# The sort's hits of rank and slot: a PSUM tile and three products in place of an SBUF tile and one

## The chip, the cores and the metric

One Trainium2 chip, one core of it. The metric is the device time of one execution in microseconds; the number given is the median of three runs. One further execution was taken by the hardware profiler, and all durations of single instructions below are from that one.

## What is computed

A graph network of two layers over 12,500 nodes with 128 features and 200,000 edges of 8 relations, then a layer norm. The edges are sorted by their destination. Each layer is

```
W = einsum('rb,bio->rio', comp, basis)
xw = einsum('ni,rio->nro', x, W)
msgs = xw[src, et]
seg = dst * N_REL + et
summed = segment_sum(msgs, seg);  cnt = segment_sum(1, seg)
mean = summed / maximum(cnt, 1)
h_new = relu(mean.reshape(N_NODES, N_REL, HIDDEN).sum(axis=1) + x @ root + bias)
h = h_new + h
```

and the output is `_layernorm(x + h)`. All values are float32.

## The kernel before

The edges are cut into 1,563 tiles of 128, and eight tiles make a quad (196 quads). **Layer 0** (the loop `for o in range(NG - 3)`) works on a quad per iteration. GpSimd issues one indirect DMA for each tile (`gather`, L806), which fetches the 128 rows of `x` that the edges of this tile name; a few tiles (`SINGLES`) are fetched row by row from the SyncE queue instead. The ring of row tiles holds seven quads, and gathers are issued five quads ahead of the iteration that uses them. TensorE multiplies the rows with one-hot matrices of destination and weight (`means`, L1364), ScalarE copies the sums out, TensorE multiplies with the relations' weights (`product`, L1396) and places the rows in blocks of 128 nodes (`place`, L1427). **Layer 1** gathers rows of a table `y_d` that layer 0 has written.

In layer 1, 62 of the 196 quads (`ROUTED`, NR = 62) are not fetched by eight gathers but picked out of SBUF by one-hot matmuls, and only edges that find no room there are fetched by one gather for the quad. The lists for that are made in layer 0 by a counting sort, **the sort** of this text: 62 steps, one in each iteration from 96 on. The profile has them between 975 and 1601 us. A step handles 8 tiles of 128 edges. Every edge belongs to one of 32 groups, and each group has 32 slots (CAP). In an iteration the step's parts stand in this order on VectorE, behind the one-hot matrices of the quad (L1270, L1278):

- `ranks_of(x)`, L1666 to L1674: TensorE has left in the PSUM tile `ct`, 256 columns of it, how many earlier edges each group had (`earlier_of`, L1643 to L1645). L1666 and L1667 take from this the rank of each edge in its group, L1668 to L1670 mark those with no room, L1671 writes the **hits**, a one where slot number equals rank (8 tiles by 32 slots), and L1674 multiplies the hits with three values of the edge (8 by 3 by 32) into `v`.
- `lefts_of(x - 1)`, L1683 to L1686: the edges with no room, for the step before. It reads eight columns of `ct` behind the counts.
- `groups_of(x + 1)`, L1626 to L1630: the one-hot groups of the next step.

TensorE's part of the iteration ends with `earlier_of`, which writes `ct` anew, and `slots_of` (L1700, L1706), which multiplies the groups with `v` and the left-overs with their values into the PSUM tile `y`. VectorE's L1666 of the next iteration is queued behind all that VectorE has before it and needs the new `ct`.

The order on every engine is the order in which the code calls these functions. A planner (`Plan.add`) puts waits on semaphores in between, from the cells that each instruction reads and writes; a read of a PSUM tile counts as a write of it there. An instruction of VectorE waits for an earlier one of VectorE only where one of its cells asks for it. Nearly all small SBUF tiles of the sort lie in one large tensor, so the profile calls them all `arena`; `cols`, the column numbers that the comparisons use, lies in PSUM.

The lines that matter for the prediction are those of `ranks_of`.

Of the kernel before, what the change touches and what calls it, by code (L numbers as in the profile page):

```python
# [9 lines left out]
F16 = mybir.dt.float16  # L10
# [4 lines left out]
ALU = mybir.AluOpType  # L15
# [415 lines left out]
def ordered_path(  # L431
# [25 lines left out]
    nc = tc.nc  # L457
    P = 128
# [11 lines left out]
    Q = 8  # L470
# [23 lines left out]
    CAP = 32  # L494
# [101 lines left out]
    def part_of(n, *cell):  # L596
        nonlocal free_at
        free_at += n
        assert free_at <= at
        sort_c.append(cell)  # L600
        return arena[:, free_at - n:free_at], cell
# [3 lines left out]
    val_b = part_of(NV * 3, "val")  # L605
# [5 lines left out]
    v_b = [part_of(Q * 3 * CAP // 2, "v", i) for i in range(2)]  # L611
    h_at = free_at
    left_hot_b = [part_of(Q * P // 2, "left_hot", i) for i in range(2)]
    j_b = part_of(Q * CAP // 2, "j")
    count_b = part_of(Q * NGR, "count")
    rank_b, lv_b, top_b = part_of(Q, "rank"), part_of(Q, "lv"), part_of(Q, "top")
    lo_b = [part_of(CAP // 2, "lo", i) for i in range(2)]
# [37 lines left out]
    cols = bank[:, :P].bitcast(F16)  # L655
# [31 lines left out]
    def vec(emit, reads=(), writes=()):  # L687
        plan.add("DVE", emit, reads, writes)
# [20 lines left out]
    def in_turn(emits):  # L709
        def emit():  # L710
            for e in emits:
                last = e()
            return last

        return emit
# [812 lines left out]
    val = val_b[0].bitcast(F16).rearrange("p (n k v) -> p n k v", k=Q, v=6)  # L1528
# [77 lines left out]
    def hots_of(x):  # L1606
        o, oc = oh_b[x % 3]
        return o.bitcast(F16).rearrange("p (t g) -> p t g", g=NGR), oc
# [8 lines left out]
    def flags(x):  # L1617
        f, c = fl_b[x % 2]
        f = f.bitcast(F16)
        return f[:, 1:Q + 1], f[:, 11:11 + Q + 2], f[:, 22:22 + Q], f, c  # L1620
# [11 lines left out]
    def counts_in(b):  # L1632
        return b.rearrange("p t d -> p (t d)")[:, :Q * NGR].rearrange("p (t g) -> p t g", g=NGR)

    def before_in(b):
        return b.rearrange("p t d -> p (t d)")[:, Q * NGR:Q * NGR + Q]

    def earlier_of(x):
        b, bc = ct_b
        reads, emits = [tri_b[1], one_b[1]], []  # L1640

        def sums(at_b, one, two):
            nc.tensor.matmul(at_b, tri, one, start=True, stop=False)  # L1643
            nc.tensor.matmul(at_b[:, 1:], every, two[:, :Q - 1], start=False, stop=False)
            return nc.tensor.matmul(at_b[:, 5:], every, two[:, :Q - 5], start=False, stop=True)  # L1645

        if x < NR:
            (o3, oc), (r2, rc) = hots_of(x), run2(x)
            reads += [oc, rc]
            emits.append(lambda: sums(counts_in(b), o3[:, 1:], r2))  # L1650
        if x > 0:
            f0, _, f2, _, fc = flags(x - 1)
            reads.append(fc)
            emits.append(lambda: sums(before_in(b), f0, f2))
        pe(in_turn(emits), reads, [bc])

    def ranks_of(x):
        (o3, oc), (vv, vc), (jt, jc), (ct, cc) = hots_of(x), v_b[x % 2], j_b, count_b
        f0, f1, f2, fw, fc = flags(x)
        b, bc = ct_b  # L1660
        c3 = ct.rearrange("p (t g) -> p t g", g=NGR)
        b3 = counts_in(b)
        j3 = jt.bitcast(F16).rearrange("p (t c) -> p t c", t=Q)
        v4 = vv.bitcast(F16).rearrange("p (t v c) -> p t v c", t=Q, v=3)
        rk, rc = rank_b
        vec(lambda: nc.vector.tensor_tensor(c3, b3, o3[:, 1:], op=ALU.mult), [bc, oc], [cc])  # L1666
        vec(lambda: nc.vector.tensor_reduce(rk, c3, axis=AX.X, op=ALU.add), [cc], [rc])  # L1667
        vec(lambda: nc.vector.tensor_scalar(f0, rk, float(CAP), None, op0=ALU.is_ge), [rc], [fc])  # L1668
        vec(lambda: nc.vector.tensor_tensor(f1[:, 2:], f0, fw[:, :Q], op=ALU.add), [], [fc])
        vec(lambda: nc.vector.tensor_tensor(f2, f1[:, 2:], f1[:, :Q], op=ALU.add), [], [fc])  # L1670
        vec(lambda: nc.vector.tensor_tensor(  # L1671
            j3, cols[:, None, :CAP].to_broadcast([P, Q, CAP]), rk.unsqueeze(2).to_broadcast([P, Q, CAP]),
            op=ALU.is_equal), ["cols", rc], [jc])
        vec(lambda: nc.vector.tensor_tensor(  # L1674
            v4, j3[:, :, None, :].to_broadcast([P, Q, 3, CAP]),
            val[:, x, :, :3].unsqueeze(3).to_broadcast([P, Q, 3, CAP]), op=ALU.mult), [jc, val_b[1]], [vc])

    def lefts_of(x):
        f0, _, _, _, fc = flags(x)
        b, bc = ct_b  # L1680
        (lv, lc), (h, hc), (top, tc_) = lv_b, left_hot_b[x % 2], top_b
        h3 = h.bitcast(F16).rearrange("p (t c) -> p t c", t=Q)
        vec(lambda: nc.vector.scalar_tensor_tensor(lv, before_in(b), 1.0, f0, op0=ALU.add, op1=ALU.mult),  # L1683
            [bc, fc], [lc])
        vec(lambda: nc.vector.tensor_tensor(top, top, lv, op=ALU.max), [lc], [tc_])
        vec(lambda: nc.vector.tensor_tensor(  # L1686
            h3, cols[:, None, 1:P + 1].to_broadcast([P, Q, P]), lv.unsqueeze(2).to_broadcast([P, Q, P]),
            op=ALU.is_equal), ["cols", lc], [hc])
# [520 lines left out]
    def sup(q):  # L2209
        return (q * Q + G) // (2 * G) - 1  # L2210
# [104 lines left out]
    for o in range(NG - 3):  # L2315
# [17 lines left out]
        if 0 <= at_x - 1 < NR:  # L2333
            ranks_of(at_x - 1)
# [22 lines left out]
        if len(tables) > 4 and (TABLE <= o < SORT - 2 or o >= SORT + NR + 4):  # L2357
            a, b = tables.pop(0)(pt_b)
# [11 lines left out]
        for i in range(2):  # L2370
            if turned_to:
                here = pt_b
                a, b = turned_to.pop(0)
            elif tables and o >= TABLE and (i == 0 or len(tables) > 6 or o > NG - 16):
# [3 lines left out]
                a, b = tables.pop(0)(here)  # L2378
# [88 lines left out]
    for q in range(NQ):  # L2467
# [48 lines left out]
        for i in range(2):  # L2516
# [14 lines left out]
            elif i == 0:  # L2531
                for j in [late] * (0 <= late < FULL) + [q] * (q >= FULL):
                    if opened_by(j)[1]:
                        a, b = finish(1, sup(j))
# [11 lines left out]
def kernel(  # L2546
# [18 lines left out]
    flag = ctx.enter_context(tc.tile_pool(name="flag", bufs=1))  # L2565
    bad = flag.tile([1, 1], I32, name="bad")
    plan = ordered_path(tc, bad, x, src, dst, et, basis, comp, root, bias, out)
    every = [mybir.EngineType.PE, mybir.EngineType.Activation, mybir.EngineType.DVE, mybir.EngineType.Pool,
             mybir.EngineType.SP]
# [36 lines left out]
```

## Time and profile before

| | |
|---|---|
| runs, median of 3 | 3381.97 us (3380.82 to 3383.55) |
| profiled execution: its own time | 3385.05 us |
| profiled execution: span, first to last instruction | 3383.1 us |
| granted TensorE clock, mean of the span | 0.911 |
| layer 0's gathers: first start, last end | 4.58 us, 1950.34 us |
| the sort: first L1674, last L1674 | 977.3 us, 1592.5 us |

The profiled execution took 3.08 us more than the median of the runs, and 1.95 us more than its own span. Times in rows are microseconds from the start of the span, and durations are microseconds unless ns is said. A row of a group of instructions gives line, engine, operation, what it writes and reads with the shapes (partitions x elements, type), the count, then the busy time and the mean duration of one in ns, then the idle time of the engine ahead of them and what ended it. A row of the timeline gives start, duration, engine, line, operation and operands, and in brackets the idle time ahead of it.

### The profile page before, as it was taken

The numbers are of one execution on the slowest core, as the hardware profiler recorded it, in microseconds if no ns is written. First come the engines' busy times: TensorE is split into PE (matmuls) and PEld (weight loads), VectorE is DVE, ScalarE is ACT, GpSimd is POOL, SyncE is SP. The second block draws the span as 40 slices with busy tenths as digits, with TensorE's granted clock in tenths as the row PEclk, the third lists the DMA queues.
The fourth block names the chain that finished last, engine by engine and source line by source line (L and its number), as shares of the span: only waits on it lengthen the run. The fifth ranks groups of instructions, "written<-read, shape, count | busy, mean of one in ns | idle before, by whom it ended". The sixth has DMA issues, their size and how long they took to land.

```text
span 3383.1 us, 73915 instructions
## 1 busy us (share of the span) xinstructions
PE 2766.1 (82%) x27537; PEld 2228.2 (66%) x27537; DVE 2270.8 (67%) x6302; ACT 644.9 (19%) x1627; POOL 2547.9 (75%) x2677
## 2 busy tenths in 40 slices
PE   6777667877667777777776739999999999999995
PEld 4565565656566666766565627777777777777774
DVE  6665454463367888888333238888888888888884
ACT  1211112222122222222222211111111111111110
POOL 7777777777777777777777777777777777777775
PEclk8999879888888888888988879999999999999997
DMA  4242223443322232222333232233223322333222
GB/s 138 56 59 64 57 77 113 132 130 95 89 82 81 75 89 76 82 77 82 115 105 89 88 101 73 72 84 85 78 78 84 84 78 78 84 85 82 78 78 61
DMA packets 171649, 289.03 MB, mean 85 GB/s; under 512 B 66163, under 2 KB 102813, under 8 KB 171285
## 3 DMA queue, kind: packets, MB, share of 16 engines
q0 software_dynamic: 85408, 175.09, 20.3%
q1 hardware_dynamic: 47146, 50.19, 5.0%
q10 hardware_dynamic: 38731, 58.99, 4.9%
q8 instruction: 218, 3.57, 0.5%
q14 instruction: 146, 1.20, 0.1%
HBM read 218.35 MB, written 65.70 MB: 84 GB/s over the span
## 4 chain that ended last, share of the span: by engine, by line
PE 43%; POOL 40%; issue 13%; DVE 2%; DMA 2%; ACT 1%; POOLq 0%; ACTq 0%; SPq 0%; DVEq 0%
POOL rows L806 40%; PE pt L1918 11%; PE y L1938 9%; PE po L1938 7%; PE po L1958 3%; PE s L2059 3%; PE ct L2026 2%; PE s L1364 2%; PE y L1396 1%; DMA rows<-in_x_dram,idx 1%; PE s L2061 1%; DVE dm L1270 1%; PE s L2063 1%; DVE arena L999 1%; PE pt L1495 0%
## 5 line engine op out<-in xcount | busy, mean ns | idle before, releaser
L806 POOL DMA_INDIRECT rows<-in_x_dram,idx x1539 | 1476.8, 960 | 471.3 <-issue 463.5
L806 POOL DMA_INDIRECT rows<-y_d,idy x1067 | 1010.4, 947 | 325.1 <-issue 316.6
L1364 PE MATMUL s<-dm,rows 128*128 128x128 f32 x3078 | 531.6, 344 | 379.6 <-DMA rows<-in_x_dram,idx 351.8
L1364 PEld LDWEIGHTS s<-dm,rows 128*128 128x128 f32 x3078 | 495.2, 252 | 441.1 <-issue 228.1
L1270 DVE TENSOR_SCALAR dm<-cols,kr,w 128x128 f32<-128x128 f16 x1563 | 525.1, 400 | 194.7 <-PE pt L1495 54.8
L1396 PE MATMUL y<-w_sb,sT 128*128 128x128 f32 x3136 | 438.6, 299 | 46.4 <-ACT sT L704 46.4
L1396 PEld LDWEIGHTS y<-w_sb,sT 128*128 128x128 f32 x3136 | 424.6, 217 | 56.4 <-ACT sT L704 55.2
L1918 PE MATMUL pt<-arena,dm 128*32 128x128 f32 x12152 | 391.3, 275 | 2.8 <-DVE dm L1868 2.1
L704 ACT ACTIVATE sT<-s 128x512 f32<-128x512 f32 x391 | 212.3, 594 | 824.8 <-PE s L1364 824.8
L1918 PEld LDWEIGHTS pt<-arena,dm 128*32 128x32 f32 x12152 | 324.6, 110 | 55.2 <-issue 43.0
L1938 PE MATMUL y<-arena,dm 128*128 128x304 f32 x620 | 229.6, 452 | 35.1 <-DVE arena L1885 35.1
L1229 DVE TENSOR_SCALAR sT<-cols,kr,w 128x32 f32<-128x32 f16 x1040 | 238.1, 300 | 7.4 <-PE s L2063 7.3
L1868 DVE TENSOR_TENSOR dm<-arena,cols 128x768 f32<-128x768 f16 x248 | 231.3, 933 | 4.1 <-DMA dm<-sc_d 3.7
L1448 DVE TENSOR_TENSOR po<-po,carry 128x128 f32<-128x128 f32 x98 | 28.8, 294 | 296.9 <-PE pt L1495 104.2
L1938 PE MATMUL po<-arena,dm 128*128 128x304 f32 x620 | 210.3, 421 | 0.0
L704 ACT ACTIVATE dm<-pt 128x256 f32<-128x256 f32 x248 | 95.4, 385 | 578.2 <-PE pt L1918 533.6
L1495 PE MATMUL pt<-w_sb,arena 128*128 128x512 f32 (+1 forms) x326 | 174.5, 618 | 26.3 <-ACT y_row L704 14.9
L704 ACT ACTIVATE y_row<-pt 128x512 f32<-128x512 f32 x165 | 98.5, 597 | 417.8 <-PE pt L1495 153.3
L1938 PEld LDWEIGHTS y<-arena,dm 128*128 128x128 f32 x620 | 102.9, 189 | 88.4 <-DVE arena L1885 35.3
L1885 DVE TENSOR_SCALAR arena<-cols,comp_sb 128x608 f32<-128x608 f16 x155 | 134.9, 902 | 36.1 <-DMA arena<-y_d,arena 36.0
L1938 PEld LDWEIGHTS po<-arena,dm 128*128 128x128 f32 x620 | 118.4, 191 | 41.3 <-issue 0.7
L1885 DVE TENSOR_SCALAR arena<-cols,sel 128x608 f32<-128x608 f16 x155 | 134.8, 902 | 0.0
(327 smaller groups left out, 3583.5 us busy)
## 6 DMA issues: line engine op xcount, KB each, us to landing
hw_SP<-in_x_dram SPq DMA_DIRECT2D x3072, 0.5 KB
y_d<-y_row ACTq DMA_DIRECT2D x96, 512.0 KB
rows<-in_x_dram,idx POOLq DMA_INDIRECT x1539
rows<-y_d,idy POOLq DMA_INDIRECT x1067
arena<-lo_d SPq DMA_DIRECT2D x62, 256.0 KB
x_g<-in_x_dram SPq DMA_DIRECT2D x24, 512.0 KB
h_d<-arena ACTq DMA_DIRECT2D x96, 64.0 KB
out_dram<-x_g SPq DMA_DIRECT2D x12, 512.0 KB
```

Of the source, the lines that this page charges most:

```text
L704: act(lambda: nc.scalar.activation(out_t, in_t, AF.Copy), reads, writes)
L806: ins.append(nc.gpsimd.indirect_dma_start(out=t[:, i - q * Q, :], out_offset=None, in_=table_t, in_offset=bass.IndirectOffsetOnAxis(ap=ids ...
L1229: vec(in_turn([lambda i=i: nc.vector.tensor_scalar(t[:, i, :], cols[:, :2 * K], kr[:, i0 + i:i0 + i + 1], w[:, i0 + i:i0 + i + 1], op0=ALU ...
L1270: emits.append(lambda i=i: nc.vector.tensor_scalar(t[:, i - q * Q, :wide], cols[:, :wide], ids[:, i:i + 1], w[:, i:i + 1], op0=ALU.is_equa ...
L1364: last = nc.tensor.matmul(s_b[i // 4][0][:, i % 4, :], t[:, i, :] if one is None else one[0], d[:, i, :], start=True, stop=True)
L1396: last = nc.tensor.matmul(y[:m], t[:, r, :nt, :].rearrange("p t k -> p (t k)"), w_sb[:, 0, r, :], start=(r == 0), stop=(r == R - 1))
L1495: pe(lambda: nc.tensor.matmul(hb[:n].rearrange("p r d -> p (r d)"), hT[:, j * P:j * P + n], w_sb[:, 1, k * H:(k + 1) * H, :].rearrange("p ...
L1868: emits = [lambda: nc.vector.tensor_tensor(o[:, :3 * n].rearrange("p (j c) -> p j c", j=3), bits[:, None, u * n:(u + 1) * n].to_broadcast( ...
L1885: vec(lambda v=v, o=o: nc.vector.tensor_scalar(o, segs_p, sg[:, v:v + 1], sg[:, NTL + v:NTL + v + 1], op0=ALU.is_equal, op1=ALU.mult), ["n ...
L1918: last = nc.tensor.matmul(b[k * CAP:(k + 1) * CAP, x, :], o[:n, c:c + CAP], hT[:n, j * P:(j + 1) * P], start=jj == 0, stop=jj == SIZE[g] - 1)
L1938: last = nc.tensor.matmul(b.rearrange("p t d -> p (t d)")[:, :SEG], g[:, x * P:(x + 1) * P], o[:, k * SEG:(k + 1) * SEG], start=v == 0, st ...
L1958: pe(in_turn([lambda r=r: nc.tensor.matmul(b[:NW, 0, :], t_s[:, r * NW:(r + 1) * NW], w_sb[:, 1, r, :], start=r == 0, stop=r == R - 1) for ...
```

## The change

The hits are no longer written to a tile of their own in SBUF as 16-bit floats. They are written into the PSUM tile `ct`, over the 256 columns of the counts, which L1666 has read by then, as 32-bit floats (`hits_in`). The product of the hits with the three values is made by three VectorE instructions of 8 by 32 elements each, one for each value, that read the hits from PSUM, where before one instruction of 8 by 3 by 32 read them from SBUF. `v` is the same as before. The SBUF tile of the hits is gone from `arena`, and the sort's tiles behind it lie 128 words lower.

```
-    j_b = part_of(Q * CAP // 2, "j")
...
+    def hits_in(b):
+        return b.rearrange("p t d -> p (t d)")[:, :Q * CAP].rearrange("p (t c) -> p t c", t=Q)
...
-        (o3, oc), (vv, vc), (jt, jc), (ct, cc) = hots_of(x), v_b[x % 2], j_b, count_b
+        (o3, oc), (vv, vc), (ct, cc) = hots_of(x), v_b[x % 2], count_b
...
-        j3 = jt.bitcast(F16).rearrange("p (t c) -> p t c", t=Q)
+        j3 = hits_in(b)
...
             j3, cols[:, None, :CAP].to_broadcast([P, Q, CAP]), rk.unsqueeze(2).to_broadcast([P, Q, CAP]),
-            op=ALU.is_equal), ["cols", rc], [jc])
-        vec(lambda: nc.vector.tensor_tensor(
-            v4, j3[:, :, None, :].to_broadcast([P, Q, 3, CAP]),
-            val[:, x, :, :3].unsqueeze(3).to_broadcast([P, Q, 3, CAP]), op=ALU.mult), [jc, val_b[1]], [vc])
+            op=ALU.is_equal), ["cols", rc], [bc])
+        vec(in_turn([lambda i=i: nc.vector.tensor_tensor(
+            v4[:, :, i, :], j3, val[:, x, :, i:i + 1].to_broadcast([P, Q, CAP]), op=ALU.mult) for i in range(3)]),
+            [bc, val_b[1]], [vc])
```

The following rows are VectorE's queue in the middle of the sort, from the read of the counts to the start of the left-overs' part; `x3` or `x2` at a row's end is a count of equal rows, and `s_DVE` is the semaphore on which VectorE waits for an earlier instruction of its own. Before:

```order
L1666 TENSOR_TENSOR arena<-ct,arena 128x256 [waits s_PE]
L1667 TENSOR_REDUCE arena<-arena 128x8 [waits s_DVE]
L1668 TENSOR_SCALAR arena<-arena 128x8 [waits s_DVE]
L1669 TENSOR_TENSOR arena<-arena 128x8 [waits s_DVE]
L1670 TENSOR_TENSOR arena<-arena 128x8 [waits s_DVE]
L1671 TENSOR_TENSOR arena<-cols,arena 128x256
L1674 TENSOR_TENSOR arena<-arena 128x768 [waits s_DVE]
L1683 SCALAR_TENSOR_TENSOR arena<-ct,arena 128x8
L1685 TENSOR_TENSOR arena<-arena 128x8 [waits s_DVE]
```

The same place in the changed kernel, whose lines are two higher from here on:

```order
L1668 TENSOR_TENSOR arena<-ct,arena 128x256 [waits s_PE]
L1669 TENSOR_REDUCE arena<-arena 128x8 [waits s_DVE]
L1670 TENSOR_SCALAR arena<-arena 128x8 [waits s_DVE]
L1671 TENSOR_TENSOR arena<-arena 128x8 [waits s_DVE]
L1672 TENSOR_TENSOR arena<-arena 128x8 [waits s_DVE]
L1673 TENSOR_TENSOR ct<-cols,arena 128x256
L1676 TENSOR_TENSOR arena<-ct,arena 128x8x32 [waits s_DVE]
L1676 TENSOR_TENSOR arena<-ct,arena 128x8x32 x2
L1685 SCALAR_TENSOR_TENSOR arena<-ct,arena 128x8 [waits s_DVE]
L1687 TENSOR_TENSOR arena<-arena 128x8 [waits s_DVE]
```

The hits (L1671 before, L1673 after) have another destination; one product with two operands in `arena` has become three with one operand in `ct`; and the first instruction of the left-overs (L1683 before, L1685 after) waits for the products, because both read `ct`. No instruction has moved past another, and the other engines' queues are the same in both kernels.

## The prediction

> **What bounds the kernel now.** I read the first part of the page, then the chain, then the waits of GpSimd.
>
> ```profile
> PE 2766.1 (82%) x27537; PEld 2228.2 (66%) x27537; DVE 2270.8 (67%) x6302; ACT 644.9 (19%) x1627; POOL 2547.9 (75%) x2677
> ...
> PE 43%; POOL 40%; issue 13%; DVE 2%; DMA 2%; ACT 1%; POOLq 0%; ACTq 0%; SPq 0%; DVEq 0%
> ...
> L806 POOL DMA_INDIRECT rows<-in_x_dram,idx x1539 | 1476.8, 960 | 471.3 <-issue 463.5
> L806 POOL DMA_INDIRECT rows<-y_d,idy x1067 | 1010.4, 947 | 325.1 <-issue 316.6
> ```
>
> By busy time TensorE looks like the bound, but the chain gives 53% of the span to POOL and "issue", and POOL's 75% is not slack. Layer 0's gathers (first row) are busy 1476.8 us and idle 471.3 ahead of them: 1948 us, which is all of layer 0 (its last gather ends at 1950.3). The waits of GpSimd tell what that idle time is:
>
> ```profile
> POOL rows L806 <- issue: 780.1, 2559, 0.3
> ```
>
> There were 2559 pauses of 0.3 us, none longer, and none that waits for another engine. A gather takes 0.95 us, its successor starts 0.30 later, and so it goes for the whole of layer 0. TensorE waits for them there, not they for TensorE. In the window of the sort, for instance:
>
> ```profile
> PE s L1364 <- DMA rows<-in_x_dram,idx: 131.6, 50, 4.5
> ```
>
> So **layer 0 is as long as its gathers, and whatever lengthens one lengthens layer 0**. Now the same group in two windows, the sort (975 to 1600 us) and what follows it in layer 0 (1600 to 1950 us), with the smallest, median and largest duration in ns below:
>
> ```profile
> L806 POOL DMA_INDIRECT rows<-in_x_dram,idx x487 | 478.1, 982 | 148.5 <-issue 147.6 <-PE y L1706 0.6 <-PE ct L1645 0.3
> L806 POOL DMA_INDIRECT rows<-in_x_dram,idx x281 | 265.4, 945 | 85.7 <-issue 85.1 <-PE ct L1495 0.3 <-DMA y_d<-y_row 0.3
> L806 POOL DMA_INDIRECT rows<-in_x_dram,idx x487: 940/945/1719, 974.2 to 1599.5; - x163
> L806 POOL DMA_INDIRECT rows<-in_x_dram,idx x281: 940/945/957, 1599.5 to 1949.4; - x141
> ```
>
> The median is 945 ns in both, but in the sort the mean is 982 and one gather took 1719. Some gathers are held up there: 487 x (982 - 945) ns = **18.0 us**. The timeline shows by what. First GpSimd, then VectorE at the same time:
>
> ```profile
> 1168.66 0.94 POOL L806 DMA_INDIRECT rows<-in_x_dram,idx  x1 [0.30 <-issue]
> 1169.90 1.71 POOL L806 DMA_INDIRECT rows<-in_x_dram,idx  x1 [0.30 <-issue]
> 1171.92 0.94 POOL L806 DMA_INDIRECT rows<-in_x_dram,idx  x1 [0.30 <-issue]
> ...
> 1169.84 0.96 DVE L1674 TENSOR_TENSOR arena<-arena 128x768 f16<-128x768 f16 x1
> 1170.71 0.16 DVE L1683 SCALAR_TENSOR_TENSOR arena<-ct,arena 128x8 f32<-128x8 f32 x1
> 1170.91 0.17 DVE L1685 TENSOR_TENSOR arena<-arena 128x8 f32<-128x8 f32 x1
> 1170.99 1.22 DVE L1686 TENSOR_TENSOR arena<-cols,arena 128x1024 f16<-128x1024 f16 x1
> ```
>
> L1674 began 0.06 before the second gather and ended at 1170.80; this gather ended at 1171.61, 0.81 later. A gather that is not held takes 0.945, so it seems to need something in its first 0.13 us that L1674 holds to its end. The third gather starts 0.93 into L1686, which has 0.29 still to run, and takes 0.94 all the same. This pattern holds in all of the sort. In 43 of the 62 steps L1674 covers the first 0.13 us of a gather; all 43 are lengthened (0.99 to 1.72 us), each ending 0.81 to 0.83 after L1674. The first and the last of them:
>
> ```profile
> 977.92 1.13 POOL L806 DMA_INDIRECT rows<-in_x_dram,idx  x1 [0.30 <-issue]
> 977.27 0.96 DVE L1674 TENSOR_TENSOR arena<-arena 128x768 f16<-128x768 f16 x1
> ...
> 1592.88 1.36 POOL L806 DMA_INDIRECT rows<-in_x_dram,idx  x1 [0.30 <-issue]
> 1592.46 0.96 DVE L1674 TENSOR_TENSOR arena<-arena 128x768 f16<-128x768 f16 x1
> ```
>
> The other 19 steps have no such overlap and no long gather. Which instructions hold gathers up? L1674 reads both operands from SBUF (`arena`). L1686, L1671 and L1666 read one from PSUM (`cols` or `ct`) and one from SBUF, and no gather that started under them is longer than 0.96 us. For the form that the change uses, `ct` with `arena`:
>
> ```profile
> 1297.93 0.42 DVE L1666 TENSOR_TENSOR arena<-ct,arena 128x256 f32<-128x256 f32 x1 [0.58 <-PE y L1706]
> 1298.14 0.94 POOL L806 DMA_INDIRECT rows<-in_x_dram,idx  x1 [0.30 <-issue]
> ```
>
> The Trainium skill, SBUF — State Buffer, "Who interferes with whom", has a rule for this: a VectorE instruction with two SBUF inputs contends with a GpSimd instruction that reads SBUF, and one with at most one SBUF input, outside certain fast modes, does not. By that rule the stalls of L1674 would go; the rows above agree with both halves of it. The same section also infers the contrary for this very case: a tensor_tensor should not hold up the making of descriptors, since that needs the write side. By that the sum would be nothing; the 1.71 us gather speaks against it.
>
> **The change part by part.** These rows price VectorE's part:
>
> ```profile
> L1666 DVE TENSOR_TENSOR arena<-ct,arena 128x256 f32<-128x256 f32 x62 | 26.1, 421 | 96.3 <-PE y L1706 79.0 <-PE ct L1645 10.2 <-issue 7.1
> L1671 DVE TENSOR_TENSOR arena<-cols,arena 128x256 f16<-128x256 f16 x62 | 25.9, 418 | 0.0
> L1674 DVE TENSOR_TENSOR arena<-arena 128x768 f16<-128x768 f16 x62 | 59.6, 961 | 2.1
> L1629 DVE TENSOR_TENSOR arena<-arena 128x256 f16<-128x256 f16 x62 | 18.1, 292 | 2.1
> L1448 DVE TENSOR_TENSOR po<-po,carry 128x128 f32<-128x128 f32 x97 | 28.5, 294 | 296.8 <-PE pt L1495 104.2 <-PE po L1427 83.1 <-PE ct L1495 81.2
> L1472 DVE SCALAR_TENSOR_TENSOR arena<-po,wide 128x128 f32<-128x128 f32 x97 | 27.9, 287 | 1.5
> ```
>
> *Hits to PSUM.* L1448 writes PSUM and L1472 SBUF, with the same inputs and size: 294 and 287 ns. So the hits stay at about 0.42 us.
>
> *Three products for one.* Each has 256 elements and the operands of L1666: 421 ns. No wait stands between them, and VectorE then starts an instruction before the last one ends:
>
> ```profile
> 1294.33 2.63 DVE L1270 TENSOR_SCALAR dm<-cols,kr,w 128x128 f32<-128x128 f16 x8
> ```
>
> Eight of 0.40 in 2.63 are (2.63 - 0.40) / 7 = 0.32 from start to start, an overlap of 0.08. Three products: 0.42 + 2 x 0.34 = 1.10 us for 0.96, that is +0.14. *The added wait:* L1683 now starts 0.87 after L1674 (1169.84, 1170.71); changed, it waits for the last product to end, some +0.04 behind it as behind other waits, so it starts 1.14 after the first. Together **+0.27 us a step, 17 us on VectorE**. Bounds: each product at 292 ns as in L1629 makes a step 0.14 shorter; each as long as L1674 itself, 0.96 and with no overlap, makes it 2.05 longer. I take the value from L1666, whose operands are the products' own.
>
> *What hides it.* VectorE waits 96.3 us ahead of L1666, 1.55 us a step, for TensorE's last matmuls of the iteration. Behind the lengthened place stand L1685, L1686, the groups, then the next quad's one-hots; who waits for them is TensorE, which itself waits for gathers (131.6 us above), and rows are gathered five quads, some 50 us, ahead. After the change a step is 0.29 us shorter (18.0 / 62) and VectorE's part 0.27 longer, so 1.55 shrinks to 1.0. That is a mean; the waits themselves in the window of the sort are
>
> ```profile
> DVE arena L1666 <- PE y L1706: 79.0, 39, 3.8
> DVE arena L1666 <- PE ct L1645: 10.2, 1, 10.2
> DVE arena L1666 <- issue: 7.1, 4, 2.0
> ```
>
> so in 62 - 44 = 18 steps there is no wait ahead of L1666 today; the lead of the gathers has to cover these, as it does now. If that cover were gone the cost would be the 17 us.
>
> *What goes.* The stalls of L1674: -18.0 us. *What is left:* L1629 and L1630 also read twice from `arena`, 292 ns each, and can hold a gather for 0.292 - 0.13 - 0.05 = 0.11 us at most. Today they sit where they hold none; moved by 0.27 us they will meet some. From nothing to 124 x 0.11 = 14 us; with the phase open, a tenth of 124 at half of 0.11, +0.7 us. L1685, 170 ns, is too short to cover the 0.13 + 0.05. *Layer 1* starts when the last of layer 0 is there and moves as a whole.
>
> Sum: 3385.05 - 18.0 + 0.7 = 3367.7 for the profiled execution; the median of the runs is 3.08 lower: **3364.7 us**.
>
> **Rivals.**
>
> *The stalls stay.* What holds the gather is not the second SBUF operand but something that the products keep, the read of the values or the write of `v`. Then nothing is gained, and the hold grows by 0.14 us in 43 steps: 3382 to 3388, within 0.2%. L1666 and L1686, which read and write `arena` as the products will, speak against it. Chance 0.05. (The inference of the Trainium skill in SBUF — State Buffer, "Who interferes with whom", leads to the lower end of this by another way.)
>
> *A part of the gain is eaten*, by L1629 and L1630 if they lock to a bad phase, or because the 18 steps without a wait hold up TensorE for longer than the lead of the gathers covers: 5 to 14 us given back, 3370 to 3379. For it: gathers and VectorE are locked to one another through TensorE, so phases repeat. Against it: the lead of 50 us. Chance 0.12, of which 0.04 is within 0.2%.
>
> *VectorE becomes the bound, slower.* Place: the steps of the sort. It decides once the products' part costs over 1.55 us a step more, since then VectorE has no wait left at today's pace. At the far end, 0.96 each, it costs 2.05: 62 x (2.05 - 1.55) = +31 us, 3413. Its busy time is near enough to a step to take it seriously:
>
> ```profile
> 975.00:1600.00 625.00, 467.67 (x3668) 424.67 (x3666) 510.52 (x1455) 149.41 (x426) 476.81 (x487) 0.84 0.29 81
> ```
>
> The third pair is VectorE, 510.52 of 625. Against it: the row of L1666 itself. Chance 0.05.
>
> **How the numbers follow.** The forecast has 0.78. Its own spread is the runs' (3380.8 to 3383.6) and the 0.7: 3361 to 3368. With the range to 3373, which takes in a part of the second rival, about 0.8 is inside; the lower end, 3360, allows for all of 18.0 and a low median. 0.2% is 6.8 us, about what a measurement of this kernel can tell from no change. Faster by more: 0.78 + 0.08 = 0.86; within: 0.05 + 0.04 = 0.09; slower: 0.05.
>
> **What would show it.** The gathers' mean in the sort falls from 982 to about 946 ns, and the largest from 1719 to under 1.06 us; last gather of layer 0 at about 1933 in place of 1950. Products of about 0.42 us, three of them in 1.1. VectorE's idle time ahead of L1668 (L1666 now) about 62 us in place of 96. Wrong would be: long gathers that end 0.81 after the third product; GpSimd pauses that wait for TensorE; a wait of TensorE for VectorE in the place of that for rows.

## The result, and the profile after

The changed kernel took **3362.84 us** (median of four runs, 3361.46 to 3363.84), the kernel before 3382.76 beside it: a ratio of **0.9941, with a 95% interval of 0.9928 to 0.9953**. The prediction was 3364.7, and 17.3 us less than before; measured are 19.9 us. A later comparison of the same two kernels gave 3380.4 and 3363.72, a ratio of 0.9953 (0.9937 to 0.997), 16.7 us less. So both measurements are as near to the forecast as they are to one another.

The page of the changed kernel, with the lines that answer to those of before (its line numbers are one lower up to L1632 of the kernel before, and two higher in the sort's later lines and behind them):

```profile
PE 2746.4 (82%) x27537; PEld 2208.7 (66%) x27537; DVE 2283.4 (68%) x6426; ACT 644.8 (19%) x1627; POOL 2529.0 (75%) x2677
...
L805 POOL DMA_INDIRECT rows<-in_x_dram,idx x1539 | 1458.5, 948 | 471.5 <-issue 463.8
L805 POOL DMA_INDIRECT rows<-y_d,idy x1067 | 1009.9, 947 | 325.2 <-issue 315.4
```

Layer 0's gathers are busy for 1458.5 us, before for 1476.8: 18.3 us less, with the same idle time. Layer 1's are as they were. In the window of the sort, 975 to 1583 us now, the group and its smallest, median and largest duration are:

```profile
L805 POOL DMA_INDIRECT rows<-in_x_dram,idx x488 | 460.7, 944 | 148.9 <-issue 148.3 <-PE y L1708 0.6
L805 POOL DMA_INDIRECT rows<-in_x_dram,idx x488: 940/944/994, 974.5 to 1582.8; - x163
```

The mean has fallen from 982 to 944 ns and the largest from 1719 to 994. GpSimd's gathers still wait for next to nobody: 2556 pauses that no other engine ends, none over 0.3 us.

```profile
POOL rows L805 <- issue: 779.2, 2556, 0.3
```

VectorE's rows in the sort, and the timeline of one step, GpSimd first and VectorE below:

```profile
L1676 DVE TENSOR_TENSOR arena<-ct,arena 128x256 f16<-128x256 f32 x186 | 67.4, 419 | 2.1
L1673 DVE TENSOR_TENSOR ct<-cols,arena 128x256 f32<-128x256 f16 x62 | 26.4, 426 | 0.0
L1668 DVE TENSOR_TENSOR arena<-ct,arena 128x256 f32<-128x256 f32 x62 | 26.1, 421 | 64.6 <-PE y L1708 51.5 <-PE ct L1647 9.4 <-issue 3.1
```

```profile
1173.10 0.94 POOL L805 DMA_INDIRECT rows<-in_x_dram,idx  x1 [0.30 <-issue]
1174.35 0.94 POOL L805 DMA_INDIRECT rows<-in_x_dram,idx  x1 [0.31 <-issue]
...
1172.43 0.43 DVE L1673 TENSOR_TENSOR ct<-cols,arena 128x256 f32<-128x256 f16 x1
1172.90 1.09 DVE L1676 TENSOR_TENSOR arena<-ct,arena 128x256 f16<-128x256 f32 x3
1174.02 0.17 DVE L1685 SCALAR_TENSOR_TENSOR arena<-ct,arena 128x8 f32<-128x8 f32 x1
1174.30 1.22 DVE L1688 TENSOR_TENSOR arena<-cols,arena 128x1024 f16<-128x1024 f16 x1
```

The gather at 1173.10 starts 0.20 into the products, which go on for 0.89 us, and takes its 0.94. The left-overs' part starts 1.12 us after the first product (0.87 before).

Where the 21.1 us of the two profiled spans went (3383.1 to 3362.0): the last gather of layer 0 ended at 1932.24 in place of 1950.34, which is 18.1 us. The other 3.0 lie in layer 1, and most of that at its end, in the chain of the last quads. The last two groups of 16 matmuls in that chain took, first before, then after:

```profile
3342.45 6.74 PE s L2083 x16
...
3366.89 6.33 PE s L2083 x16
```

```profile
3324.06 5.41 PE s L2085 x16
...
3346.95 5.19 PE s L2085 x16
```

That is 2.5 us less for the same 32 matmuls. In the second comparison's profile of the changed kernel the last of these groups took less again:

```profile
3348.32 3.51 PE s L2085 x16
```

So two profiles of one and the same kernel differ there by 1.7 us. The runs of the kernel before spread from 3378.0 to 3385.2 us over the two comparisons, and its profiled execution, at 3385.05, is near the upper end. The 3.0 us are within that spread, and nothing here ties them to the change.

The experiments below ran on four chips. On three of them the kernel before took 4884 to 4886 us, and GpSimd waited for TensorE there, so that gathers did not set the time. Of these runs single gathers are read below, whose usual duration is the same there (0.945), and no ratio is taken for the worth of a stall.

```profile
POOL rows L805 <- PE ct L2028: 956.8, 116, 55.0
POOL rows L805 <- issue: 706.0, 2307, 2.9
POOL rows L805 <- PE s L1363: 374.8, 81, 37.4
```

These are GpSimd's waits in the first run with one product from PSUM: some 1330 us of waiting for TensorE, where the two kernels above have next to none.

### The profile page after: what moved, and what is told of

Same layout as the page of the kernel before. It is cut to its first block, busy times and chain, and to the rows that moved or that the text cites. A ratio compares the mean times of both kernels' runs of the same rounds, so it can differ in the third digit from the quotient of the medians.

```text
span 3362.0 us, 74039 instructions
## 1 busy us (share of the span) xinstructions
PE 2746.4 (82%) x27537; PEld 2208.7 (66%) x27537; DVE 2283.4 (68%) x6426; ACT 644.8 (19%) x1627; POOL 2529.0 (75%) x2677
## 4 chain that ended last, share of the span: by engine, by line
PE 44%; POOL 37%; issue 12%; DVE 3%; DMA 2%; ACT 1%; POOLq 0%; ACTq 0%; SPq 0%; DVEq 0%
POOL rows L805 37%; PE pt L1920 11%; PE y L1940 9%; PE po L1940 8%; PE po L1960 3%; PE s L2061 3%; PE ct L2028 2%; PE s L1363 2%; DMA rows<-in_x_dram,idx 1%; PE y L1395 1%; DVE dm L1269 1%; PE s L2063 1%; PE pt L1494 1%; PE s L2065 1%; DVE arena L998 1%
## 5 line engine op out<-in xcount | busy, mean ns | idle before, releaser
L805 POOL DMA_INDIRECT rows<-in_x_dram,idx x1539 | 1458.5, 948 | 471.5 <-issue 463.8
L1363 PE MATMUL s<-dm,rows 128*128 128x128 f32 x3078 | 520.1, 338 | 376.9 <-DMA rows<-in_x_dram,idx 348.1
L1363 PEld LDWEIGHTS s<-dm,rows 128*128 128x128 f32 x3078 | 483.3, 246 | 440.1 <-issue 211.3
```

Of the source, the lines that this page charges most:

```text
L805: ins.append(nc.gpsimd.indirect_dma_start(out=t[:, i - q * Q, :], out_offset=None, in_=table_t, in_offset=bass.IndirectOffsetOnAxis(ap=ids ...
L1363: last = nc.tensor.matmul(s_b[i // 4][0][:, i % 4, :], t[:, i, :] if one is None else one[0], d[:, i, :], start=True, stop=True)
```

## The experiments

The theory: an instruction of VectorE that reads both operands from SBUF holds up a gather that starts under it, until it ends. The chief rivals: that the cutting into three short instructions freed the gathers; that the write of `v` or the read of the values holds them. A gather is counted below as lying under an instruction if it starts more than 0.05 us after it and its first 0.13 us end before it does (why 0.05 is told in the last section). The stalls of a run are the sum, over all gathers of its sort, of what each took beyond 0.945 us; in the profile before they come to 18.4 us.

**One product, read from PSUM.** The hits stay in PSUM, the product is one instruction again:

```
-        vec(in_turn([lambda i=i: nc.vector.tensor_tensor(
-            v4[:, :, i, :], j3, val[:, x, :, i:i + 1].to_broadcast([P, Q, CAP]), op=ALU.mult) for i in range(3)]),
-            [bc, val_b[1]], [vc])
+        vec(lambda: nc.vector.tensor_tensor(
+            v4, j3[:, :, None, :].to_broadcast([P, Q, 3, CAP]),
+            val[:, x, :, :3].unsqueeze(3).to_broadcast([P, Q, 3, CAP]), op=ALU.mult), [bc, val_b[1]], [vc])
```

> Hits in PSUM as after the change, but one product of 768 elements, read from PSUM. Theory: one SBUF operand, so no stall however long the instruction is: gathers of the sort at 0.945 us in the mean, 3363, the same as the change; VectorE 0.14 us a step shorter, and that is worth nothing. Rival (the cutting into three is what counts): stalls as before, 3382.

It was run three times, each time on a chip where GpSimd waits for TensorE; the expectations of the other two:

> The kernel of the run with one product from PSUM once more, since on the chip of the first four runs every kernel, the one before included, took 45% longer and GpSimd waited for TensorE, so that gathers did not set the time. Theory: no gather is held by the product, whatever its length; the same time as the change, 0.994 of before, VectorE's product at 0.96 us. A few gathers are held by the 0.29 us additions of two SBUF operands behind it, under 0.1 us each, 2 us in all. Rival (the cutting into three is what counts): 0.999 to 1.001 of before.

> One product of 768 from PSUM, on a chip where before takes about 3380. Theory: no gather is held by it; the change's own time, 0.994 to 0.996 of before, though VectorE has 0.14 us a step less to do. A few gathers are held by the additions of two SBUF operands, 2 us in all. Rival (the cutting into three is what counts): 0.999 to 1.001.

The first run's product, the sort's gathers, and one gather (second row from the end) under one product (last row):

```profile
L1676 DVE TENSOR_TENSOR arena<-ct,arena 128x768 f16<-128x768 f32 x62 | 59.4, 958 | 2.1
L805 POOL DMA_INDIRECT rows<-in_x_dram,idx x490: 938/944/1037, 1282.5 to 2077.8; - x164
1341.02 0.95 POOL L805 DMA_INDIRECT rows<-in_x_dram,idx  x1 [0.30 <-issue]
1340.25 0.96 DVE L1676 TENSOR_TENSOR arena<-ct,arena 128x768 f16<-128x768 f32 x1
```

The product is as long as L1674 was. In the first run 45 gathers lie under it, and the longest of those took 0.953; in the other two runs 46 and 38, with longest 0.957 and 0.961. So it is not the cutting, and neither the write of `v` nor the read of the values. Nor is it that the hits became 32-bit numbers with the move: L1688 of the same run reads 16-bit `cols` from PSUM beside `arena`, and the longest of the 44 gathers under it took 0.947. The gathers of 0.98 to 1.04 us in this run's row lie under the additions L1628 and L1629 behind, which read twice from `arena`: 1.8 us of stalls in all, the 2 us that the second expectation names.

The times were 1.0117 (1.0089 to 1.0144), 1.0098 (1.0059 to 1.0137) and 1.0088 (1.0057 to 1.012) of before. That this form is as fast as the change where gathers set the time follows from its gathers, but was not measured.

**Three products, read from SBUF.** The kernel before, with the hits in SBUF, and only its product cut into three:

```
-        vec(lambda: nc.vector.tensor_tensor(
-            v4, j3[:, :, None, :].to_broadcast([P, Q, 3, CAP]),
-            val[:, x, :, :3].unsqueeze(3).to_broadcast([P, Q, 3, CAP]), op=ALU.mult), [jc, val_b[1]], [vc])
+        vec(in_turn([lambda i=i: nc.vector.tensor_tensor(
+            v4[:, :, i, :], j3, val[:, x, :, i:i + 1].to_broadcast([P, Q, CAP]), op=ALU.mult) for i in range(3)]),
+            [jc, val_b[1]], [vc])
```

> Hits in SBUF as before the change, but three products, each of 256 elements with two operands in SBUF. Theory (an instruction with two SBUF operands holds what a gather needs in its first 0.13 us): the stalls are back. If a waiting gather cannot get in between two products that follow one another without a wait, the hold is 1.1 us and the sort loses about 62 x (1.1 - 0.18)^2 / 2.5 = 21 us to it: 3384. If it can get in, a hold is 0.42 us, at most 0.25 us of stall, and the loss about 4 us: 3367. Rival (it was the cutting into three short instructions that freed the gathers, not the PSUM operand): no gather over 1.0 us in the sort, 3363.

> The kernel of the run with three products from SBUF once more. Theory, with what its first profile showed (a waiting gather gets in between two products, so that it is held for 0.25 us at most): about 50 gathers held by 0.17 us each, 8 us in the sort in place of 18, so 0.997 of before, between before and the change. Rival (the cutting into three is what counts): 0.994. Rival (only the operand counts, and a row of such products holds as one): 1.000.

> Three products with both operands in SBUF, on such a chip. Theory (each holds a gather for 0.25 us at most, and a waiting gather gets in between): about 45 gathers held by 0.17 us each, 8 us in place of 18, so 10 us faster than before, 0.997. Rival (only the cutting counts): 0.994 to 0.996 and no gather over 1.0 us. Rival (the operands alone count, three hold as long as one): 1.000.

The first run's products, the sort's gathers, and one step's gathers over its products:

```profile
L1674 DVE TENSOR_TENSOR arena<-arena 128x256 f16<-128x256 f16 x186 | 68.1, 421 | 2.1
L806 POOL DMA_INDIRECT rows<-in_x_dram,idx x490: 939/945/1189, 1284.2 to 2051.4; - x164
1301.53 0.94 POOL L806 DMA_INDIRECT rows<-in_x_dram,idx  x1 [0.30 <-issue]
1302.78 1.14 POOL L806 DMA_INDIRECT rows<-in_x_dram,idx  x1 [0.30 <-issue]
...
1302.00 1.10 DVE L1674 TENSOR_TENSOR arena<-arena 128x256 f16<-128x256 f16 x3
```

The second gather starts under the third product, which ends at 1303.10, and ends 0.82 after it, as those under L1674 did. Of 53 gathers that lay under the three products, 50 were lengthened, by 0.25 us at most; 48 of 50 and 47 of 49 in the repeats. No gather was held for longer than one product of 0.42 us allows: 0.42 less the 0.05 and the 0.13 us is 0.24. So a waiting gather gets its turn where one product ends and the next has begun to run. The stalls of the sort sum up to 8.3, 7.8 and 8.4 us in the three runs, twice the 4 us of the first expectation. The 18.4 us of the kernel before are from a profile in which gathers set the time; on a chip of this kind it was not profiled, so how much of the difference is the cutting's is not measured. The operand decides whether a gather is held, the length of one instruction for how long. The times, 1.0032, 1.0024 and 1.0026 of before (the intervals begin at 1.0003 to 1.0012), are not the 0.997 of the expectations; GpSimd waits for TensorE in these runs, so they say nothing on stalls.

**The product from SBUF twice.** The kernel before, with L1674 repeated into a tile that nothing reads:

```
+    dup = keep([P, 1 * Q * 3 * CAP // 2], F32, "dup").bitcast(F16).rearrange("p (n t v c) -> n p t v c", n=1, t=Q, v=3)
...
-        vec(lambda: nc.vector.tensor_tensor(
-            v4, j3[:, :, None, :].to_broadcast([P, Q, 3, CAP]),
-            val[:, x, :, :3].unsqueeze(3).to_broadcast([P, Q, 3, CAP]), op=ALU.mult), [jc, val_b[1]], [vc])
+        vec(in_turn([lambda o=o: nc.vector.tensor_tensor(
+            o, j3[:, :, None, :].to_broadcast([P, Q, 3, CAP]),
+            val[:, x, :, :3].unsqueeze(3).to_broadcast([P, Q, 3, CAP]), op=ALU.mult) for o in (v4, dup[0])]),
+            [jc, val_b[1]], [vc, "dup"])
```

> The kernel before with its product of 768 elements from SBUF made twice, the second time into a tile that nothing reads. Theory: the hold is 1.84 us in place of 0.96, longer than the 1.25 us from one gather to the next, so nearly every step has a held gather, on the mean by about 1.84 - 0.18 - 0.62 = 1.04 us: 62 x 1.04 = 64 us of stalls in place of 18, so about 3428, and the longest gather at about 2.6 us. Rival (the long gathers come from something else in these steps): the 0.88 us more of VectorE a step is within its 1.55 us of waiting, so 3382 to 3385.

The longest gather took 1.72 us and not 2.6, though nearly every step holds one now (59 gathers in the 62 steps; in the profile before 43):

```profile
L806 POOL DMA_INDIRECT rows<-in_x_dram,idx x491: 939/945/1720, 1280.4 to 2049.6; - x164
1374.62 1.56 POOL L806 DMA_INDIRECT rows<-in_x_dram,idx  x1 [0.31 <-issue]
...
1373.54 0.96 DVE L1675 TENSOR_TENSOR arena<-arena 128x768 f16<-128x768 f16 x1
1374.41 0.95 DVE L1675 TENSOR_TENSOR dup<-arena 128x768 f16<-128x768 f16 x1
```

The gather at 1374.62 waits for the second product (it ends 0.82 after that). But a gather that is held by the first is not held by the second as well, or there would be some over 1.72. So doubling the work does not double the hold, and the expectation was wrong in that. The whole is 14.9 us of stalls, where 64 were expected. Its time, 1.0003 (0.9978 to 1.0029) of before, tells nothing here.

**Two SBUF operands, written to PSUM.** The changed kernel, with one more instruction in each step behind the left-overs:

```
+        h_b, h_bc = left_hot_b[(x - 1) % 2]
+        vec(lambda: nc.vector.tensor_tensor(
+            b.rearrange("p t d -> p (t d)"), h.bitcast(F16)[:, :4 * P], h_b.bitcast(F16)[:, :4 * P], op=ALU.mult),
+            [hc, h_bc], [bc])
```

> The changed kernel with one more VectorE instruction in each step, behind the left-overs: 512 products of two SBUF operands written to PSUM (over counts that are done with), about 0.69 us. Theory in the form 'the second SBUF read is what holds the gather': every gather whose first 0.13 us lies under it is lengthened, to 0.945 + 0.51 = 1.46 us at most, 62 x (0.69 - 0.18)^2 / 2.5 = 6 us in all: 3369. In the form 'it takes a write to SBUF as well': no long gathers. On VectorE the 0.73 us more a step is within its 1.04 us of waiting, so without stalls 3363. Rival: no long gathers and 3363.

The added row, the sort's gathers, and one gather with the instruction over it:

```profile
L1692 DVE TENSOR_TENSOR ct<-arena 128x512 f32<-128x512 f16 x62 | 43.5, 701 | 2.1
L805 POOL DMA_INDIRECT rows<-in_x_dram,idx x497: 938/944/1428, 1284.1 to 2081.6; - x166
1484.89 1.43 POOL L805 DMA_INDIRECT rows<-in_x_dram,idx  x1 [0.30 <-issue]
1484.80 0.70 DVE L1692 TENSOR_TENSOR ct<-arena 128x512 f32<-128x512 f16 x1
```

All 20 gathers that lie under it are lengthened, to 0.99 to 1.43 us, each ending 0.81 to 0.82 after it; of the 46 under the products from PSUM in the same run, none. It writes nothing to SBUF. So the second read from SBUF is enough to hold a gather. The time, 1.0078 (1.0053 to 1.0103) of before on a chip where GpSimd waits for TensorE, tells nothing of stalls.

**More products, read from PSUM.** The changed kernel's three products made twice and four times (the second with `dup[1]` and `dup[2]` too):

```
+    dup = keep([P, 1 * Q * 3 * CAP // 2], F32, "dup").bitcast(F16).rearrange("p (n t v c) -> n p t v c", n=1, t=Q, v=3)
...
-        vec(in_turn([lambda i=i: nc.vector.tensor_tensor(
-            v4[:, :, i, :], j3, val[:, x, :, i:i + 1].to_broadcast([P, Q, CAP]), op=ALU.mult) for i in range(3)]),
-            [bc, val_b[1]], [vc])
+        vec(in_turn([lambda i=i, o=o: nc.vector.tensor_tensor(
+            o[:, :, i, :], j3, val[:, x, :, i:i + 1].to_broadcast([P, Q, CAP]), op=ALU.mult) for o in (v4, dup[0]) for i in range(3)]),
+            [bc, val_b[1]], [vc, "dup"])
```

> The changed kernel with its three products from PSUM made twice, the second time into a tile that nothing reads: +1.0 us of VectorE a step. Theory (VectorE waits 1.04 us a step ahead of the read of the counts, and gathers are issued some 50 us ahead): the cover just holds, 0.994 to 0.995 of before, with the wait ahead of the read of the counts nearly gone. Rival (VectorE's time is on the path, since many steps have no wait): +1.0 us in each of the 62 steps, 62 us, 1.012.

> The changed kernel with its three products made four times: +3.0 us of VectorE a step, 2.0 us more than VectorE's waiting covers. Theory: 62 x 2.0 = 122 us of delay, of which the lead of the gathers (seven quads of rows, some 50 us) takes up a part once, and TensorE makes that part good behind the sort, where it waits for rows: +70 us on the change, 1.015 of before, with GpSimd waiting for TensorE in the second half of the sort. If the lead does not help: +122 us, 1.030. If VectorE's time does not matter at all: 0.994.

> The changed kernel with its three products made four times, on such a chip: +3.0 us of VectorE a step, 2.0 us more than its 1.04 us of waiting ahead of the read of the counts. Theory: 62 x 2.0 = 122 us of delay, of which the lead of the gathers takes up some 50 us once: +70 us on the change, 1.015 of before, with GpSimd waiting for TensorE late in the sort and no gather held. If the lead does not help: +122 us, 1.030. If VectorE's time does not matter: 0.995.

All three fell on chips where GpSimd waits for TensorE: 1.011 (1.0057 to 1.0163), 1.0087 (1.0055 to 1.0119) and 1.0085 (1.0058 to 1.0111) of before. There VectorE waits some 4 us a step ahead of the read of the counts (247.7 us over the 62 steps in the first run with one product), so 3 us more of work is covered. The question, how much VectorE can take where gathers set the time, was not answered. The last run tells of gathers, though:

```profile
L1677 DVE TENSOR_TENSOR dup<-ct,arena 128x256 f16<-128x256 f32 x558 | 189.7, 411 | 0.0
L1669 DVE TENSOR_TENSOR arena<-ct,arena 128x256 f32<-128x256 f32 x62 | 26.2, 423 | 76.9 <-remote 51.8 <-PE s L1363 18.2 <-PE ct L1648 4.6
```

The twelve products run for 4.06 us on end in each step, 182 gathers lie under them, and the longest took 0.957.

**The change once more**, beside the kernel before, on the fourth chip, where gathers set the time:

> The changed kernel itself, beside the kernel before on the same chip, since on the chips of the last runs all kernels took 45% longer and TensorE kept GpSimd waiting. If gathers set the time of layer 0 on this chip (before at about 3382): 0.994, as measured first. If TensorE does (before at about 4886): the freed gathers are worth nothing, since GpSimd waits for TensorE anyway, so by the theory 1.000; the other kernels with the hits in PSUM took 1.008 to 1.012 of before there, those with the hits in SBUF 1.000 to 1.003, so a rival for that state is that the PSUM hits themselves cost TensorE time: 1.010.

0.9953 (0.9937 to 0.997), from 3380.4 to 3363.72, with none of the 44 gathers under the products held: the first case of the three.

## Why the prediction was right

*What bounds layer 0.* Right. The gathers lost 18.3 us of busy time, their idle time stayed (471.5 us, 471.3 before), and the last one of layer 0 ended 18.1 us earlier.

*What holds a gather.* Right, and shown. Whether it is held goes with the second SBUF operand in every form that was run: one product or three, an SBUF or a PSUM destination. The rule of the Trainium skill in SBUF — State Buffer, "Who interferes with whom", that a VectorE instruction with two SBUF inputs contends with a GpSimd instruction that reads SBUF, agrees with this. By the inference in the same section, that a tensor_tensor does not hold up the making of descriptors, one would not expect it; the prediction set it against the 1.71 us gather, and here L1674 held gathers up to 0.77 us, and an instruction that writes no SBUF up to 0.48. Whether that refutes the inference is open: a gather is held in its first 0.13 us only, it also has its list of row numbers (`idx`) to read, and no run tells which part of its work is held.

One sentence on the 43 steps is not right, that the other 19 have no such overlap. In three of them L1674 covers the first 0.13 us of a gather as well, but began only 0.005 to 0.032 us ahead of it, and these gathers took 0.94. Where a gather was held, L1674 had begun at least 0.056 ahead. The sum is not touched by it, since it goes by the mean of all gathers.

*The price on VectorE.* Hits 0.426 us (0.42 forecast), products 0.419 each and 1.09 in a row (0.42 and 1.10), the left-overs' part 0.25 later (0.27). The lower bound is not what its own row gives: three products at 292 ns with the overlap of 0.08, and the wait of 0.04 behind them, put the left-overs' part 0.11 earlier than today, not 0.14. The wait ahead of the read of the counts is 64.6 us in place of 96.3 (62 forecast).

*The cover.* The gathers wait for nobody in the sort, so the cover held for the 0.25 us more a step; how far it reaches is open.

*The rest.* The additions of two SBUF operands were put at 0.7 us; the stalls left in the sort are 0.4 us in the first profile, and 0.6 in the second comparison's. The long gathers among them, four and eight, all lie under the first addition, L1628, so the size came out by where the additions happen to fall.

*The sum.* 17.3 us forecast, 19.9 and 16.7 measured; the profiled spans differ by 21.1, of which 18.1 is the mechanism's, and 3.0 lie in layer 1, for which the sum had no term and which are within the spread of the runs. That the median came 2.6 us under the forecast in one comparison and 0.6 over it in the other is scatter of this kind.

The rivals fell: the stalls did not stay, hardly anything of the gain was eaten (the 0.4 to 0.6 us above), and VectorE did not become the bound.

## What to carry to other kernels

Where GpSimd issues indirect DMAs back to back, look at the spread of their durations, not the mean: long ones name the VectorE instruction whose end they follow at a fixed distance. An operand moved from SBUF to PSUM frees them, and the product took no longer for it (0.958 us as one instruction from PSUM, 0.961 from SBUF). The cutting into three was not needed for that, and made the products 0.13 us longer in a row. Cutting an instruction that must read two SBUF operands into short ones bounds each hold, for some more of VectorE's time. Ask first that nothing else sets the time: on chips where GpSimd waited for TensorE, none of the forms that shorten the stalls was faster than the kernel before.

## What was not expected of the hardware

In the sort, a held gather gets its turn between two VectorE instructions that follow one another without a wait: three products of 0.42 us hold for 0.25 us at most, and two of 0.96 for no more than one. It isn't so everywhere. In the profile before, one gather ahead of the sort started under a cast, L1583, and ended 1.39 us after it, with a second cast behind the first:

```profile
708.01 1.99 POOL L806 DMA_INDIRECT rows<-in_x_dram,idx  x1 [0.30 <-issue]
...
707.62 0.99 DVE L1583 CAST arena<-arena 128x496 f16<-128x496 int32 x1
708.65 0.99 DVE L1584 CAST arena<-near 128x496 f16<-128x496 f32 x1
```

That gather also suggests that two SBUF operands are not the only way to hold one: a cast reads a single tensor. Plainer is another cast from SBUF to SBUF, in the changed kernel at the start of layer 1: the gather that starts under it takes 1.45 us and ends 0.82 after it:

```profile
1949.32 1.45 POOL L805 DMA_INDIRECT rows<-y_d,idy  x1 [0.30 <-DMA y_d<-y_row]
...
1948.93 1.03 DVE L2001 CAST kr<-idx 128x1664 f32<-128x1664 int32 x1
```

Which instructions with one tensor operand hold a gather was not tested here; the sort's reduction L1667, from `arena` to `arena`, held none of the 16 that lay under it.

The hold goes both ways. In four steps of the profile before, a gather began between 0.01 us ahead of L1674 and 0.032 behind its start. None of these gathers was held; L1674 was, and took 0.98 to 1.02 us in place of 0.96, ending 0.99 after the gather's start each time. One of them:

```profile
1582.88 0.94 POOL L806 DMA_INDIRECT rows<-in_x_dram,idx  x1 [0.30 <-issue]
...
1582.86 1.02 DVE L1674 TENSOR_TENSOR arena<-arena 128x768 f16<-128x768 f16 x1
```

So the one that comes first holds the other. The shortest lead at which an instruction held a gather was 0.05 us in all runs, which is why gathers that start sooner are not counted as lying under it.

The kernel before took 3380 to 3383 us in the two comparisons with the change, and 4884 to 4886 on three chips. The granted TensorE clock was 0.91 in the first case and 0.80 in the second; why it is so much slower there is not known, nor whether it is the chip or what it was doing at the time, since each chip was used for one series only. There, every one of the seven runs with the hits in PSUM took 1.008 to 1.012 of the kernel before, and the four with the hits in SBUF 1.000 to 1.003. The difference arises in the sort and what follows it in layer 0: from the first to the last read of the counts the sort takes 776 to 796 us there with the hits in PSUM, 755 to 761 with the hits in SBUF, and layer 1 is alike (2438 to 2455 us, and 2437 to 2453). It isn't VectorE's length (the SBUF product made twice has 756), and it isn't in the order of the other engines' queues, which the change leaves as it was. The cause was not found. The change itself was not run on such a chip; going by its nearest relatives, an estimate, it would lose about one per cent there rather than gain.
